# Softmax sums of a two-layer masked attention: summing layer 1's pair tiles by accumulating DMAs, layer 0's sums in place

## The chip, the cores and the metric

The kernel runs on one core of a Trainium2 chip. The metric is the device time of one execution in microseconds (us), the median of several runs. All tensors that matter here are float32.

## What is computed

Two attention layers on 16 graphs of 1024 nodes with 256 features. Each layer normalizes its input, applies ReLU, and adds a masked multi-head attention to it. Layer 0 has 4 heads of 64, layer 1 has 8 heads of 32 and biases.

```python
h = jnp.maximum(_layernorm(x), 0.0)
q, k, v = heads(h @ Wq), heads(h @ Wk), heads(h @ Wv)      # layer 1: + bq, bk, bv
scores = jnp.einsum('bhnd,bhmd->bhnm', q, k) / sqrt(D)
scores = jnp.where(adj > 0, scores, -inf)
w = jax.nn.softmax(scores, axis=-1)
x = x + concat(einsum('bhnm,bhmd->bhnd', w, v)) @ Wo + bo
```

## The kernel before

Scores are computed transposed: keys on the 128 partitions, 512 queries in the free dimension. A **step** is one tile `p` of 128 x 4 x 512 numbers: in layer 1 four heads against one block of 128 keys, in layer 0 two heads against two blocks. A **group** is the steps that share an output: 8 steps in layer 1, 4 in layer 0. There are two groups for each half of the queries, so a graph has 16 steps in layer 0 and 32 in layer 1, and the program has 768 in all. The list of steps goes through layer 0 of graph b+1 and then layer 1 of graph b, so that one graph's projections can be computed under the other's attention. In the text that follows, a is the first step of layer 0 of graph b+1 and c the first of layer 1 of graph b.

`Stream.run` writes the order of the work by hand, one loop turn i for each step:

- `scores(st)` on PE (TensorE): four matmuls into two PSUM pairs of a ring of three.
- `weigh` on PE, two steps later: four matmuls of `v` and `p` into `po`. In an even step that holds a large unit (`k`, `q`, `values`, `end_half`) it is put off to the odd step after it.
- `exponentials(st)`: for each half of the tile DVE (VectorE) applies the mask by a minimum (L388), and ACT (ScalarE) takes the exponential (L393). The tiles of odd steps have two buffers, those of even steps three.
- units that are due at this step: parts of the normalization of the next inputs (`stats`, `norm`, `add_bias`), the transposes (`turn`), the projections (`k`, `q`, `values`), the output projection (`end_half`, which fills `py`), and pieces of the mask (`load`, `flip`, `put`, `second`). `later(i, f)` gives a unit its step.

A softmax sum is taken by PE too: `count` multiplies a tile by a matrix of ones, so that the sum over the keys stands in all partitions of its head. To spend fewer matmuls, tiles are added first. In layer 1, `count_steps` lets POOL (GpSimd) add an odd step's tile to the even one before it (L502, 128 x 2048), and the sum is counted two steps later: four counts for a group. In layer 0, `add_tiles` adds a step's two halves into a tile `t` (DVE, for the first step POOL) and POOL adds the running sum (L418); the group is counted once.

When a group ends, `end_group` sets the steps of its end: `spread` (ACT copies the sum to `s`, SP sends it to DRAM as `sd` and back as `sn`, spread over the partitions), `invert` (DVE's reciprocal `vn`, and SP's DMAs that broadcast it as `inv`), `normalize` (POOL multiplies the output by it into `cat`) and `end_half` (PE). In layer 0 these are 2, 3, 5 and 7 steps after the group's last weigh, in layer 1 they are 2, 4, 7 and 9, and for a graph's last group 2, 3, 4 and 8. The program's last group has `hurry` set and a shorter end.

[...]

Of the kernel before, what the change touches and what calls it, by code (L numbers as in the profile page):

```python
# [18 lines left out]
P = 128  # L19
# [63 lines left out]
def fast_program(ctx, tc, a, w, loads, chk):  # L83
# [14 lines left out]
    small = ctx.enter_context(tc.tile_pool(name="small", bufs=4))  # L98
# [50 lines left out]
    class Inputs:  # L149
# [6 lines left out]
        def stats(self, half, tiles=range(4)):  # L156
# [10 lines left out]
            if 3 in tiles:  # L167
                ve = small.tile([P, 4], F32, tag="ve", name=f"ve_{n}")
                nc.gpsimd.tensor_scalar_add(ve, mv[:, :, 1], EPS)
                self.rstd[half] = small.tile([P, 4], F32, tag="rstd", name=f"rstd_{n}")  # L170
# [3 lines left out]
                self.shift[half] = small.tile([P, 4], F32, tag="shift", name=f"shift_{n}")  # L174
# [76 lines left out]
    class Group:  # L251


        def __init__(self, inp, mask, qh, g, half):
# [9 lines left out]
            self.hurry = False  # L264

# [113 lines left out]
    def exponentials(st, between):  # L379
# [4 lines left out]
        st.p = pp.tile([P, 4, 512], F32, tag=f"p{odd}", bufs=2 if odd else 3, name=f"p_{st.n}")  # L384
# [44 lines left out]
    class Stream:  # L429
# [19 lines left out]
        def run(self):  # L449
# [3 lines left out]
            for i in range(n + LEAD):  # L453
# [36 lines left out]
        def count_steps(self, i, st):  # L490


            gr = st.gr
            if st.j % 2 == 0 and not (gr.hurry and st.j == NT - 2):
                return
            if gr.hurry and st.j >= NT - 2:
                if st.last:
                    self.counted(i, gr)
                gr.count(st.p, False, st.last)
            else:  # L500
                one = self.steps[i - LEAD - 1].p
                nc.gpsimd.tensor_add(one, one, st.p)  # L502
                self.later(i + 2, gr.count, one, st.j == 1, st.last)
# [7 lines left out]
        def end_group(self, i, gr):  # L511
# [82 lines left out]
    for b in range(B):  # L594
# [4 lines left out]
        steps += layer_steps(inputs[1][b], masks[b])  # L599
    steps[-1].gr.hurry = True  # L600
# [23 lines left out]
    for b in range(B - 1):  # L624
        mine, a, c = inputs[1][b], first[b + 1], second[b]
        if b == 0:

            norms(mine, 0, a + 1, a + 2, a + 4, a + 5)
            half_inputs(mine, 0, a + 6, a + 8, a + 10, a + 12)
            norms(mine, 1, a + 9, a + 10, a + 12, a + 13)  # L630
            half_inputs(mine, 1, a + 15, c + 2, c + 6, c + 4)
        else:
            norms(mine, 0, a - 10, a - 9, a - 7, a - 6)
            half_inputs(mine, 0, a - 5, a + 2, a + 4, a + 6)
            norms(mine, 1, a - 8, a - 7, a - 5, a - 4)
            half_inputs(mine, 1, a - 3, a + 8, c + 6, c + 4)
        for kt in range(NT):
            later(a + 4 + kt, masks[b].second, kt)
        if b + 2 < B:
            other, mask = inputs[0][b + 2], masks[b + 2]  # L640
            later(a + 1, open_x, b + 2, 0)
            later(a + 10, open_x, b + 2, 1)
# [9 lines left out]
        else:  # L652
            last, e = inputs[1][b + 1], c + 32
            norms(last, 0, c + 1, c + 2, c + 4, c + 5)
            half_inputs(last, 0, c + 9, c + 12, c + 14, c + 16)
            norms(last, 1, c + 9, c + 10, c + 12, c + 13)
            half_inputs(last, 1, c + 17, c + 20, e + 6, e + 4)
            for kt in range(NT):
                later(c + 8 + 2 * kt, masks[b + 1].second, kt)
# [250 lines left out]
```

## Time and profile before

| | |
|---|---|
| median of 3 runs | 3377.5 us (3376.9 to 3377.79) |
| profiled execution, own time | 3380.06 us |
| its span, first to last instruction | 3378.3 us |
| granted TensorE clock | 0.998 |
| PE busy | 3339.0 us (99%) |
| DVE busy | 2501.1 us (74%) |
| POOL busy | 2447.1 us (72%) |
| ACT busy | 2182.5 us (65%) |
| DMA queues, share of 16 engines | SP's 12.6%, POOL's 6.3% |

A line of the groups reads: source line, engine, operation, output and inputs by the program's names, shapes and count, then busy time in us and the mean of one in ns, then the idle time of the engine just before, with what ended it. A line of a timeline reads: start and duration in us, engine, source line, operation, count, and in brackets the idle time before with what ended it. PEld are the weight loads, SPq is the DMA-issuing sequencer of SP. Each float32 matmul appears as two records.

### The profile page before, as it was taken

What the parts mean: (1) busy time and instruction counts of PE and PEld (TensorE: products, weight loads), DVE (VectorE), ACT (ScalarE), POOL (GpSimd) and SP (SyncE); (2) the same over time, 40 slices, a digit from 0 to 9 for tenths busy, and PEclk for the clock granted to TensorE, in tenths of its full rate; (3) what the DMA queues carried; (4) which work ended last, traced back from release to release, by engine and by line L of the source; (5) the groups of instructions that cost most, each with busy time, mean ns of one, the idle gap of its engine ahead of it and who ended that gap; (6) DMA issues with size and microseconds to landing.
All of it is one profiled execution on the core that took longest, in us unless ns stands there. A gap on an engine that the chain in (4) does not pass through costs nothing. (4 is left out here: it accounts for less than half of the span.)

```text
span 3378.3 us, 46298 instructions
## 1 busy us (share of the span) xinstructions
PE 3339.0 (99%) x18190; PEld 1298.6 (38%) x18190; DVE 2501.1 (74%) x2664; ACT 2182.5 (65%) x2402; POOL 2447.1 (72%) x1606
## 2 busy tenths in 40 slices
PE   8999999999999999999999999999999999999998
PEld 3443333333333333333334333333343333433432
DVE  4676767767677786777867778677786777777876
ACT  5567566675666756667566675666756667665665
POOL 5577778777677766877677686777867778676776
PEclk9999999999999999999999999999999999999999
DMA  6221111212112111121221212212121111210001
GB/s 131 48 42 36 48 39 36 51 36 47 36 36 51 42 42 36 39 48 42 45 39 36 48 39 48 39 39 45 39 47 37 48 39 36 51 38 18 14 17 31
DMA packets 250738, 141.77 MB, mean 42 GB/s; under 512 B 182416, under 2 KB 217488, under 8 KB 250512
## 3 DMA queue, kind: packets, MB, share of 16 engines
q1 hardware_dynamic: 232080, 105.18, 12.6%
q0 software_dynamic: 18432, 33.56, 6.3%
q8 instruction: 144, 2.36, 0.3%
q14 instruction: 82, 0.67, 0.1%
HBM read 120.33 MB, written 18.34 MB: 41 GB/s over the span
## 5 line engine op out<-in xcount | busy, mean ns | idle before, releaser
L393 ACT ACTIVATE p<-p 128x1024 f32<-128x1024 f32 x1536 | 1615.1, 1057 | 973.8 <-DVE p L388 931.7
L388 DVE SCALAR_TENSOR_TENSOR p<-mask,ps 128x1024 f32<-128x1024 fp8e4 x1536 | 1797.0, 1215 | 583.5 <-PE ps L372 553.8
L502 POOL TENSOR_TENSOR p<-p,p 128x2048 f32<-128x2048 f32 x255 | 1161.9, 4557 | 372.2 <-PE po L405 368.3
L372 PE MATMUL ps<-qT,kT 32*128 32x512 f32 (+1 forms) x6144 | 1145.6, 631 | 7.6 <-DVE p L388 4.9
L405 PE MATMUL po<-p,v 128*32 128x512 f32 (+1 forms) x6144 | 992.4, 601 | 0.4 <-ACT o L288 0.4
L418 POOL TENSOR_TENSOR t<-t,t 128x1024 f32<-128x1024 f32 x192 | 486.2, 2532 | 389.8 <-DVE t L416 341.6
L372 PEld LDWEIGHTS ps<-qT,kT 32*128 32x128 f32 (+1 forms) x6144 | 367.7, 184 | 675.7 <-issue 305.3
L405 PEld LDWEIGHTS po<-p,v 128*32 128x32 f32 (+1 forms) x6144 | 227.8, 118 | 689.4 <-issue 529.1
L416 DVE TENSOR_TENSOR t<-p 128x1024 f32<-128x1024 f32 x192 | 325.0, 1693 | 14.6 <-POOL t L418 14.4
L278 PE MATMUL pz<-p,ones 128*32 128x512 f32 x2056 | 267.8, 593 | 0.2 <-POOL p L502 0.2
L212 PE MATMUL pq<-hT,wk 128*128 128x512 f32 x512 | 240.7, 613 | 3.1 <-ACT hT L201 3.1
L353 PE MATMUL py<-wo,cat 128*128 128x256 f32 x1008 | 237.8, 387 | 4.7 <-POOL cat L324 2.8
L241 PE MATMUL pv<-wv,hT 128*128 128x256 f32 x1024 | 237.9, 385 | 0.1
L212 PE MATMUL pq<-hT,wq 128*128 128x512 f32 x512 | 236.6, 605 | 0.0
L241 PEld LDWEIGHTS pv<-wv,hT 128*128 128x128 f32 x1024 | 189.4, 190 | 71.7 <-issue 24.0
L353 PEld LDWEIGHTS py<-wo,cat 128*128 128x128 f32 x1008 | 185.4, 190 | 80.0 <-issue 33.4
L324 POOL TENSOR_TENSOR cat<-o,inv 128x512 f32<-128x512 f32 x127 | 164.5, 1296 | 10.3 <-DMA inv<-vd 9.3
L416 POOL TENSOR_TENSOR t<-p 128x1024 f32<-128x1024 f32 x64 | 165.0, 2578 | 2.8 <-ACT p L393 2.4
L358 DVE TENSOR_TENSOR x<-py,x 128x1024 f32<-128x1024 f32 x63 | 76.4, 1213 | 118.4 <-PE py L353 118.4
L190 POOL TENSOR_TENSOR x<-x,bo 128x1024 f32<-128x1024 f32 x64 | 152.6, 2385 | 1.5 <-DMA bo<-in_bo_dram 1.4
L212 PEld LDWEIGHTS pq<-hT,wk 128*128 128x128 f32 x512 | 93.5, 192 | 145.2 <-issue 120.1
L212 PEld LDWEIGHTS pq<-hT,wq 128*128 128x128 f32 x512 | 92.2, 189 | 139.8 <-issue 138.3
(51 smaller groups left out, 1635.4 us busy)
## 6 DMA issues: line engine op xcount, KB each, us to landing
adj<-in_adj_dram POOLq DMA_DIRECT2D x128, 256.0 KB, 3.6
x<-in_x_dram SPq DMA_DIRECT2D x32, 512.0 KB
inv<-vd SPq DMA_DIRECT2D x128, 128.0 KB
inv<-vd SPq DMA_DIRECT2D x252, 64.0 KB
out_dram<-x SPq DMA_DIRECT2D x31, 512.0 KB
adjT<-adj SPq DMA_TRANSPOSE x128
sd<-s SPq DMA_DIRECT2D x64, 4.0 KB
sn<-sd SPq DMA_DIRECT2D x64, 4.0 KB
```

The source lines that it names most:

```text
L212: nc.tensor.matmul(pq[:, m, :], wt[self.layer][:, c, ts(m, P)], self.hT[half][:, c, :], start=(c == 0), stop=(c == 1),)
L241: nc.tensor.matmul(pv[:, i, :], self.hT[half][:, c, ts(i, P)], w.v[self.layer][:, c, :], start=(c == 0), stop=(c == 1),)
L278: nc.tensor.matmul(self.s[r * self.D : (r + 1) * self.D, :], w.ones[:, : self.D], p[:, r, :], start=start, stop=stop,)
L324: nc.gpsimd.tensor_mul(self.half.cat[:, self.g, :], self.ob, self.inv)
L353: nc.tensor.matmul(py[:, i, :], self.half.cat[:, c, ts(i, P)], w.o[self.layer][:, c, :], start=(c == 0), stop=(c == 1),)
L372: nc.tensor.matmul(st.ps[i // 2][:, i % 2, :], gr.inp.kT[r * D : (r + 1) * D, gr.g, ts(kt, P)], gr.inp.qT[r * D : (r + 1) * D, gr.g, ts(gr ...
L388: nc.vector.scalar_tensor_tensor(out=half, in0=gr.mask.m[:, kt, ts(gr.qh, 512)].unsqueeze(1).to_broadcast([P, 2, 512]), scalar=BIG, in1=st ...
L393: nc.scalar.activation(half, half, AF.Exp, scale=gr.scale)
L405: nc.tensor.matmul(gr.o[r * D : (r + 1) * D, :], gr.inp.v[:, kt, h * D : (h + 1) * D], st.p[:, i, :], start=(kt == 0), stop=(kt == NT - 1),)
L416: engine.tensor_add(t, st.p[:, 0:2, :], st.p[:, 2:4, :])
L418: nc.gpsimd.tensor_add(t, t, gr.t)
L502: nc.gpsimd.tensor_add(one, one, st.p)
```

## The change

Layer 1: POOL adds each odd step's tile to the even one as before. Then every second pair sum is added to the one before it by a DMA that accumulates (issued on POOL), and the result is counted six steps after its last weigh: two counts for a group. `brief` is set for a graph's last group, and for both last groups of the program: there the first two pair sums are added and the others are counted singly. Tiles of even steps have five buffers now. The end of a layer 1 group that is not brief moves to 6, 7, 9 and 11 steps.

Layer 0: `add_tiles` takes two steps at once, at odd steps, and works in the tiles themselves; `t` is gone. The end of a group moves to 4, 5, 7 and 9.

Units of the normalizations and projections, and the mask's second pass, get other steps. Small tiles have two buffers, `rstd` and `shift` four.

```diff
-        st.p = pp.tile([P, 4, 512], F32, tag=f"p{odd}", bufs=2 if odd else 3, name=f"p_{st.n}")
+        st.p = pp.tile([P, 4, 512], F32, tag=f"p{odd}", bufs=2 if odd else 5, name=f"p_{st.n}")
...
-    def add_tiles(st):
-        gr = st.gr
-        t = work.tile([P, 2, 512], F32, tag="t", bufs=3, name=f"t_{st.n}")
-        engine = nc.vector if st.j else nc.gpsimd
-        engine.tensor_add(t, st.p[:, 0:2, :], st.p[:, 2:4, :])
-        if st.j:
-            nc.gpsimd.tensor_add(t, t, gr.t)
-        gr.t = t
+    def add_tiles(one, two):
+        a, b = one.p[:, 0:2, :], one.p[:, 2:4, :]
+        nc.vector.tensor_add(a, a, b)
+        engine = nc.vector if one.j else nc.gpsimd
+        engine.tensor_add(b, two.p[:, 0:2, :], two.p[:, 2:4, :])
+        nc.gpsimd.tensor_add(a, a, b)
+        if one.j:
+            nc.gpsimd.tensor_add(a, a, one.gr.t)
+        one.gr.t = a
...
-                one = steps[i - 1] if 1 <= i <= n else None
-                if one and one.gr.layer == 0:
-                    add_tiles(one)
+                if i % 2 and 3 <= i <= n and steps[i - 2].gr.layer == 0:
+                    add_tiles(steps[i - 3], steps[i - 2])
...
-            else:
+            elif j % 2:
                 one = self.steps[i - LEAD - 1].p
                 nc.gpsimd.tensor_add(one, one, st.p)
-                self.later(i + 2, gr.count, one, st.j == 1, st.last)
+                if gr.hurry:
+                    self.later(i + 2, gr.count, one, j == 1, False)
+                elif gr.brief and j > 4:
+                    self.later(i + 2, gr.count, one, j == 5, st.last)
+                elif j % 4 == 1:
+                    gr.pair = one
+                else:
+                    nc.gpsimd.dma_start(one, gr.pair, accum_op=ALU.add)
+                    self.later(i + 6, gr.count, one, not gr.brief and j == 3, st.last)
...
-                self.later(i + 2, gr.count_added)
-                at = 2, 3, 5, 7
+                self.later(i + 4, gr.count_added)
+                at = 4, 5, 7, 9
             else:
-                at = (2, 3, 4, 8) if gr.last else (2, 4, 7, 9)
+                at = (2, 3, 4, 9) if gr.brief else (6, 7, 9, 11)
...
         else:
-            norms(mine, 0, a - 10, a - 9, a - 7, a - 6)
-            half_inputs(mine, 0, a - 5, a + 2, a + 4, a + 6)
-            norms(mine, 1, a - 8, a - 7, a - 5, a - 4)
-            half_inputs(mine, 1, a - 3, a + 8, c + 6, c + 4)
-        for kt in range(NT):
-            later(a + 4 + kt, masks[b].second, kt)
+            norms(mine, 0, a - 15, a - 14, a - 12, a - 11)
+            half_inputs(mine, 0, a - 9, a + 2, a + 4, a + 6)
+            norms(mine, 1, a - 11, a - 10, a - 8, a - 7)
+            half_inputs(mine, 1, a - 5, a + 8, c, a + 12)
+
+        for i, kt in zip((2, 4, 8, 12, 16, 20, 24, 28), range(NT)):
+            later(c + i, masks[b + 1].second, kt)
...
-            norms(other, 0, a + 7, a + 8, a + 10, a + 11)
-            half_inputs(other, 0, a + 14, c + 10, c + 12, c + 14)
-            norms(other, 1, a + 15, c + 1, c + 3, c + 4)
-            half_inputs(other, 1, c + 15, c + 18, c + 20, c + 24)
+            if b == 0:
+                norms(other, 0, a + 8, a + 9, a + 10, a + 11)
+                half_inputs(other, 0, a + 13, c + 8, c + 10, c + 12)
+            else:
+                norms(other, 0, a + 11, a + 12, a + 13, a + 15)
+                half_inputs(other, 0, c + 1, c + 4, c + 8, c + 12)
+            norms(other, 1, c + 1, c + 2, c + 3, c + 5)
+            half_inputs(other, 1, c + (9 if b == 0 else 7), c + 16, c + 20, c + 24)
```

`norms(inp, half, ...)` gives the steps of its four pieces (statistics twice, normalization twice; the bias addition follows one step later), `half_inputs` those of `turn`, `k`, `q` and `values`. For graph 0 and for the last graphs the units move in the same way, to steps of their own.

More of the change, by code (lines that the diff above doesn't have):

```diff
@@ L97, in fast_program @@
     pp = ctx.enter_context(tc.tile_pool(name="pp", bufs=2))
-    small = ctx.enter_context(tc.tile_pool(name="small", bufs=4))
+    small = ctx.enter_context(tc.tile_pool(name="small", bufs=2))
     ps_s = ctx.enter_context(tc.tile_pool(name="ps_s", bufs=3, space=PSUM))
@@ L169, in stats @@
                 nc.gpsimd.tensor_scalar_add(ve, mv[:, :, 1], EPS)
-                self.rstd[half] = small.tile([P, 4], F32, tag="rstd", name=f"rstd_{n}")
+                self.rstd[half] = small.tile([P, 4], F32, tag="rstd", bufs=4, name=f"rstd_{n}")
                 nc.gpsimd.tensor_tensor(self.rstd[half], ve, w.mhalf, ALU.pow)
@@ L173, in stats @@
                 nc.gpsimd.tensor_scalar_mul(less, mv[:, :, 0], -1.0)
-                self.shift[half] = small.tile([P, 4], F32, tag="shift", name=f"shift_{n}")
+                self.shift[half] = small.tile([P, 4], F32, tag="shift", bufs=4, name=f"shift_{n}")
                 nc.gpsimd.tensor_mul(self.shift[half], less, self.rstd[half])
@@ L264, in __init__ @@
             self.hurry = False
+            self.brief = self.last
         def steps(self):
@@ L490, in count_steps @@
         def count_steps(self, i, st):
[L493 to L496, printed above, removed]
+            gr, j = st.gr, st.j
+            if gr.hurry and j >= NT - 2:
                 if st.last:
@@ L599, in fast_program @@
         steps += layer_steps(inputs[1][b], masks[b])
+    for st in steps[-2 * NT :]:
+        st.gr.brief = True
     steps[-1].gr.hurry = True
@@ L626, in fast_program @@
         if b == 0:
[L628 to L631, printed above, removed]
-        else:
-            norms(mine, 0, a - 10, a - 9, a - 7, a - 6)
-            half_inputs(mine, 0, a - 5, a + 2, a + 4, a + 6)
-            norms(mine, 1, a - 8, a - 7, a - 5, a - 4)
-            half_inputs(mine, 1, a - 3, a + 8, c + 6, c + 4)
-        for kt in range(NT):
-            later(a + 4 + kt, masks[b].second, kt)
+            norms(mine, 0, a + 3, a + 4, a + 6, a + 7)
+            half_inputs(mine, 0, a + 9, a + 10, a + 12, a + 14)
+            norms(mine, 1, a + 11, a + 12, a + 14, a + 15)
+            half_inputs(mine, 1, c + 1, c + 3, c + 6, c + 4)
+            for kt in range(NT):
+                later(a + 4 + kt, masks[b].second, kt)
+        else:
+            norms(mine, 0, a - 15, a - 14, a - 12, a - 11)
[4 more added lines that the diff above has]
+            later(c + i, masks[b + 1].second, kt)
         if b + 2 < B:
@@ L641, in fast_program @@
             later(a + 1, open_x, b + 2, 0)
[L642 to L646 removed]
+            later(a + 11, open_x, b + 2, 1)
+            if b == 0:
[6 more added lines that the diff above has]
+            half_inputs(other, 1, c + (9 if b == 0 else 7), c + 16, c + 20, c + 24)
             for t in range(NT):
@@ L653, in fast_program @@
             last, e = inputs[1][b + 1], c + 32
[L654 to L659, printed above, removed]
+            norms(last, 0, c + 3, c + 4, c + 6, c + 7)
+            half_inputs(last, 0, c + 9, c + 12, c + 16, c + 20)
+            norms(last, 1, c + 11, c + 12, c + 14, c + 15)
+            half_inputs(last, 1, c + 17, c + 24, e + 6, e + 4)
     stream.run()
```

## The prediction

> **What bounds the kernel now.** I read the page's busy shares first (PE 99%, DVE 74%, POOL 72%, ACT 65%; clock 0.998), then its groups:
>
> ```profile
> L388 DVE SCALAR_TENSOR_TENSOR p<-mask,ps 128x1024 f32<-128x1024 fp8e4 x1536 | 1797.0, 1215 | 583.5 <-PE ps L372 553.8
> L502 POOL TENSOR_TENSOR p<-p,p 128x2048 f32<-128x2048 f32 x255 | 1161.9, 4557 | 372.2 <-PE po L405 368.3
> L278 PE MATMUL pz<-p,ones 128*32 128x512 f32 x2056 | 267.8, 593 | 0.2 <-POOL p L502 0.2
> ```
>
> DVE and POOL wait for PE (553.8 and 368.3 us), PE for nobody. So an instruction taken from PE shortens the span as long as the other queues keep up. Do they? The timeline of a stretch without projections, PE:
>
> ```profile
> 3292.79 1.14 PE L372 MATMUL ps<-qT,kT 32*128 32x512 f32 x8
> 3293.86 1.07 PE L405 MATMUL po<-p,v 128*32 128x512 f32 x8
> 3294.85 1.57 PE L372 MATMUL ps<-qT,kT 32*128 32x512 f32 x8
> 3296.36 1.06 PE L405 MATMUL po<-p,v 128*32 128x512 f32 x8
> 3297.24 1.04 PE L278 MATMUL pz<-p,ones 128*32 128x512 f32 x8
> 3298.21 1.14 PE L372 MATMUL ps<-qT,kT 32*128 32x512 f32 x8
> ```
>
> An even and an odd step ("pair") take 5.4 us, of which the count is 0.97 (3297.24 to 3298.21). The second scores take 1.57, not 1.14: they wait for a PSUM pair. POOL's addition of such a pair takes 4.56, the DVE masks 4 x 1.15 = 4.6: three queues are within 0.8 us of each other there. With a projection (3.65 us, start to start) a pair takes 8.5.
>
> POOL, end of a batch:
>
> ```profile
> 1378.96 4.59 POOL L502 TENSOR_TENSOR p<-p,p 128x2048 f32<-128x2048 f32 x1
> 1383.48 2.42 POOL L190 TENSOR_TENSOR x<-x,bo 128x1024 f32<-128x1024 f32 x1
> 1385.99 0.29 POOL L318 TENSOR_SCALAR ok_is_ge<-sn 128x16 f32<-128x16 f32 x1
> ...
> 1387.37 4.55 POOL L502 TENSOR_TENSOR p<-p,p 128x2048 f32<-128x2048 f32 x1
> ```
>
> POOL runs without a gap there and is already late; bias addition (2.4) and tests (1.15) stand ahead of the next pair sum. DVE waits for that sum, because the odd steps' tiles have two buffers (the waits: "DVE p L388 <- POOL p L502", 27.6 us in 16 waits). Last, a softmax sum's way to the reciprocal (ACT, SP, DVE):
>
> ```profile
> 1278.66 0.56 ACT L296 COPY s<-pz 128x512 f32<-128x512 f32 x1
> ...
> 1279.25 0.49 SPq L298 DMA_DIRECT2D sd<-s  x1
> 1280.82 0.32 SPq L300 DMA_DIRECT2D sn<-sd  x1
> ...
> 1282.45 0.20 DVE L305 RECIPROCAL vn<-sn 128x8 f32<-128x8 f32 x1 [2.52 <-DMA sn<-sd]
> ```
>
> From the end of the copy to the reciprocal: 3.2 us, and DVE stood in front of it for 2.52.
>
> [...] L416 on DVE lasts 1.22 us alone and 2.27 beside POOL, 1.69 on average.
>
> **The change part by part.** A batch is 24 pairs: a to a+14 (layer 0), c to c+30 (layer 1). In a batch of the steady state (1 to 13; 208.4 us each by the starts of their scores):
>
> *Counts.* Three groups drop from 4 counts to 2, the fourth (brief) from 4 to 3: 7 x 0.97 = **6.8 us off PE**. In all 110 counts, 107 us. Most short pairs keep theirs and the projection pairs lose theirs (8.5 to 7.5).
>
> *Other steps for units and mask pieces.* PE's work is the same. Before, pair c lasted 11.05; in batch 14, where DVE isn't late, 9.38: 1.7 us that the new order removes, with about 0.4 at c+24. PE alone would then need 208.4 - 6.8 - 2.1 = 199.5.
>
> *Accumulating DMAs.* 110 issues on POOL behind the sum that they add to; the row of the adj loads says 0.62, [...] I take 0.75, bounds 0.6 to 2. Landing: the adj queue's 6.3% of 16 engines is 1.66 us per load of 512 KB read, 3.6 with the ends. Two sources of 1 MB are 4 x 1.66 + 1.9 = 8.5 us, bounds 6 to 15. The source's buffer is wanted again (five even tiles on) 11 us or more after the issue, the count comes later still: no wait at 8.5.
>
> *Layer 0 in place.* Same additions (DVE 192, POOL 256), now in clumps after odd steps; they wait for weigh, which PE has done by then. Between 0 and 1 us a batch through DVE contention; I take it inside c+2 below. SP issues as many DMAs as before, at other steps (0.3 to 1.3 us each, with gaps between them in its timeline); the small pools cost nothing, since rstd and shift keep four buffers.
>
> *What becomes late.* I followed the queues pair by pair. A mask of an odd step may start 3.5 us into a short pair, 5.9 into one with a projection; late by more than 0.5, it delays the next scores.
>
> - c+6: L0's sum is now copied at c+5 and inverted at c+6, in a short pair. Copy ends 2.5 into it (odd exponentials and hn are ahead on ACT), plus 3.2: reciprocal at 5.7, and the odd mask behind it on DVE at 5.9 instead of 3.7. A transpose (c+7) holds the third PSUM pair, so the next scores need both of its halves: 5.9 + 2.3 against 5.4: **2.8 us**. Same cause at a: 0.5.
> - c+18 to c+22: after the sum of c+17 POOL has 4.55 + 0.75 (DMA) + 1.15 (tests) + 1.95 (rstd) + 1.3 (cat) = 9.7 in a pair of 5.4: the next sum starts 4.3 late and holds the odd mask of c+21: 1.0. DVE's statistics (1.2 in each of four steps) fall into the two short pairs: 1.6 and 1.8. **4.4 us**.
> - c+28: the output projection waits for cat, behind 4.55 + 0.75 + 1.15 + 2.4 (bias) + 1.3 = 10.1 on POOL; PE is there after 6.9 + 1.07 = 8.0: **2.2 us**.
> - c+14, c+26, c+30: a short pair right after one without count: the sum ends 4.55 in, the mask could start at 3.5; 1.1 - 0.6: **0.5 each**.
> - c+2: mask piece, statistics, reciprocal and residual (0.8 + 1.2 + 0.2 + 1.2) between DVE's masks, which start 0.7 late after the additions: **1.2**.
>
> Sum 12.6. So a batch takes 199.5 + 12.6 = 212.1, **+3.7**, and 13 batches +48. The first and the last two (19 counts, 18 us) I take at 0: their short pairs without count are held by POOL (4.55 and its extras) near 5.4 as before. The profiled execution's own time is 3380.06; 3428. The median of the runs lies 2.6 below it: **3425**.
>
> **The rivals.**
>
> 1. *The queues keep up* (faster). The mechanism is the same slack at the odd mask: if waits come to less than 8.9 us a batch, the count pays. For it: before, the pairs c+22 and c+24 took both statistics and lost only 0.5, and POOL is idle 28% of the span. Against: the three POOL queues above are sums of measured rows. Half the waits: 205.8, 13 x -2.6 = -34: 3343; none at all: -134, 3243.
> 2. *The DMA lands late* (slower still). If the add costs as much as the reads, landing is some 15 us: the even masks and the counts wait 4 us or less behind seven DMAs a batch, about 6 us beyond the waits they hide: 13 x 5.7 = +74, 3500. For it: nothing before moves 1 MB[...].
> 3. *POOL pays 2 us an issue*: 7 x 1.25, a part of it in POOL's idle time: +2.5 a batch, 3458.
> 4. *No net effect*: waits of 8.9 +/- 0.5. A narrow case.
>
> **How the numbers follow.** Slower by my ledger, with the waits between 9.4 and 14: 0.60; DMA late or issue dear: 0.18; keeping up: 0.16; no effect: 0.06. A measurement of this kernel tells about 0.2% from no change. So faster 0.16, same 0.06, slower 0.78. Range 3345 to 3490: low at half the waits, high just short of a 15 us landing. The slower cases' own range is 3385 to 3490.
>
> **What would show it.** Right: L280 with some 1176 records of layer 1 in place of 2056; pairs with a projection and no count at 7.5; c+6 near 8.2 with DVE waiting for sn; py at c+28 waiting for cat; more of "DVE p <- POOL p"; PE's busy share below 99%. Wrong: PE still without waits (then near 3250), or the reciprocal ready before 4 us in c+6. DMA landings above 11 us, with even masks released by a DMA, would show rival 2; POOL's DMA row above 1 us rival 3.

## The result and the profile after

The changed kernel takes 3794.1 us (median of 4 runs, 3785.1 to 3817.8) where the kernel before takes 3377.5: a ratio of 1.124 (95% interval 1.120 to 1.129). The direction was forecast; of the 417 us only 48 were. The profiled execution took 3817.8 us, with a span of 3816.0.

From the page of the kernel after: busy shares, granted clock in slices of the span, three groups (the mask is L390 now, POOL's pair sum L503, the count L280), and the accumulating DMA with its median us from issue to landing:

```profile
PE 3505.1 (92%) x17310; PEld 1355.0 (36%) x17310; DVE 2498.3 (65%) x2664; ACT 2172.3 (57%) x2402; POOL 2508.3 (66%) x1716
...
PEclk9999989999999998999999999998999999999989
...
L390 DVE SCALAR_TENSOR_TENSOR p<-mask,ps 128x1024 f32<-128x1024 fp8e4 x1536 | 1799.7, 1214 | 997.2 <-PE ps L374 542.7
...
L503 POOL TENSOR_TENSOR p<-p,p 128x2048 f32<-128x2048 f32 x255 | 1169.9, 4607 | 401.7 <-PE po L407 332.4
...
L280 PE MATMUL pz<-p,ones 128*32 128x512 f32 (+1 forms) x1432 | 223.8, 615 | 2.2 <-POOL p L503 2.2
...
p<-p POOLq DMA_DIRECT2D x110, 1024.0 KB, 7.1
```

No engine has become the bound: every engine's share fell. PE's busy time nevertheless rose from 3339 to 3505 us, although 880 records of the count are gone. PE stands idle for 311 us (39 before), and some clock slices show 8. Before, all showed 9:

```profile
PEclk9999999999999999999999999999999999999999
```

The idle time before DVE's mask grew from 583.5 to 997.2 us, and PE's part of it did not grow (553.8 to 542.7). What else ends it, the view of waits says (engine, what it waited for, us, times, longest):

```profile
DVE p L390 <- PE ps L374: 542.7, 326, 5.0
...
DVE p L390 <- DMA p<-p: 427.1, 92, 7.2
...
PE ps L374 <- DVE p L390: 156.5, 72, 6.1
```

A new row of 427 us: the mask of an even step waits for an accumulating DMA, six times in a batch (c+12, c+16, c+20, c+24, c+28 and the next a), 4.6 us each. PE waits for the mask in turn; before, that row of the groups had 4.9 us:

```profile
L372 PE MATMUL ps<-qT,kT 32*128 32x512 f32 (+1 forms) x6144 | 1145.6, 631 | 7.6 <-DVE p L388 4.9
```

One of these waits in the timeline of the kernel after, at c+16 (start, duration):

```profile
1474.42 0.90 POOL L511 DMA_DIRECT2D p<-p  x1 [0.30 <-POOL p L503]
...
1475.55 1.14 PE L374 MATMUL ps<-qT,kT 32*128 32x512 f32 x8
...
1481.91 2.35 DVE L390 SCALAR_TENSOR_TENSOR p<-mask,ps 128x1024 f32<-128x1024 fp8e4 x2 [5.41 <-DMA p<-p]
...
1483.19 3.21 PE L374 MATMUL ps<-qT,kT 32*128 32x512 f32 x8 [2.87 <-DVE p L390]
...
1486.33 3.53 PE L407 MATMUL po<-p,v 128*32 128x512 f32 x16
```

DVE is free from 1476.5 and the scores are there at 1476.7; the buffer for the masked tile is free when the DMA lands, 7.5 us after its issue. PE waits 2.87 us. And then its work itself is slow: scores of 3.21 us where 1.14 is usual (a part of it waits for the mask's second half), two weighs of 3.53 us where 1.92 is usual. The busy time by stretches of two microseconds (sum, PE's busy time and records, granted clock, DMA share, GB/s) shows why:

```profile
1478.00:1480.00 2.00, 2.00 (x6) 1.00 0.96 197
1480.00:1482.00 2.00, 0.32 (x1) 1.00 0.79 120
1482.00:1484.00 2.00, 0.81 (x2) 0.70 0.52 93
1484.00:1486.00 2.00, 2.00 (x8) 0.50 0.03 3
1486.00:1488.00 2.00, 2.00 (x10) 0.50 0.11 36
1488.00:1490.00 2.00, 2.00 (x16) 0.60 0.52 145
1490.00:1492.00 2.00, 2.00 (x18) 1.00 0.58 91
```

Around this wait TensorE's clock record stands at 0.50 for 6.8 us (1482.78 to 1489.61). Over the span it has 394 us at half clock (15 before). PE was at work in 359 of them. If work at half clock takes twice its time, some 180 us of them are lost (an estimate, half of the 359; 3.5 before); the two weighs above took 3.53 us for 1.92.

In a batch of the steady state (1 to 13) PE's record splits the loss as follows: 27.6 us more are 17.0 of idle time, 11.3 of work slowed by half clock (half of PE's busy time at half clock) and 5.3 of longer records of scores at full clock, which the prediction's view of the second scores (1.57 us for 1.14) lets one read as waits for a PSUM pair; the missing counts take 6.0 off. Outside these batches the changed kernel loses another 79 of the 438 us between the two profiled executions. This is bookkeeping from the records: how much of the slow clock would come back as time is another question (e8).

Where it is lost, in mean us from the start of an even step's scores to those of the next even step, over batches 1 to 13 (kernels of the experiments beside it):

| pair | before | after | e1 | e4 | e9 | e18 |
|---|---|---|---|---|---|---|
| a | 6.68 | 12.03 | 6.68 | 6.68 | 6.96 | 6.98 |
| a+2 to a+14 | 75.18 | 77.59 | 79.05 | 79.04 | 76.03 | 76.03 |
| c | 11.03 | 11.32 | 11.31 | 11.32 | 9.66 | 9.67 |
| c+2 | 5.51 | 13.97 | 13.86 | 8.89 | 7.53 | 7.40 |
| c+4, c+6 | 16.99 | 15.91 | 15.86 | 15.61 | 19.19 | 15.48 |
| c+8 | 8.50 | 10.85 | 10.66 | 11.66 | 8.86 | 8.51 |
| c+10 to c+14 | 26.50 | 22.73 | 21.51 | 21.52 | 24.79 | 24.78 |
| c+16 | 5.36 | 13.56 | 7.63 | 7.63 | 5.37 | 5.37 |
| c+18 | 8.49 | 5.49 | 10.36 | 10.19 | 7.63 | 7.63 |
| c+20, c+22 | 13.84 | 19.05 | 15.71 | 17.03 | 12.98 | 12.99 |
| c+24 | 8.99 | 10.75 | 9.87 | 9.56 | 15.32 | 9.84 |
| c+26 to c+30 | 21.29 | 22.78 | 21.74 | 21.75 | 20.62 | 23.01 |
| batch | 208.38 | 236.01 | 224.23 | 220.87 | 214.95 | 207.69 |

### The profile page after: what moved, and what is told of

Its sections match the earlier page's. It is cut to its first block, busy times and chain, and to the rows that moved or that the text cites. A ratio compares the mean times of both kernels' runs of the same rounds, so it can differ in the third digit from the quotient of the medians.

```text
span 3816.0 us, 44831 instructions
## 1 busy us (share of the span) xinstructions
PE 3505.1 (92%) x17310; PEld 1355.0 (36%) x17310; DVE 2498.3 (65%) x2664; ACT 2172.3 (57%) x2402; POOL 2508.3 (66%) x1716
## 3 DMA queue, kind: packets, MB, share of 16 engines
q1 hardware_dynamic: 232080, 105.18, 11.3%
## 5 line engine op out<-in xcount | busy, mean ns | idle before, releaser
L390 DVE SCALAR_TENSOR_TENSOR p<-mask,ps 128x1024 f32<-128x1024 fp8e4 x1536 | 1799.7, 1214 | 997.2 <-PE ps L374 542.7
L503 POOL TENSOR_TENSOR p<-p,p 128x2048 f32<-128x2048 f32 x255 | 1169.9, 4607 | 401.7 <-PE po L407 332.4
L374 PE MATMUL ps<-qT,kT 32*128 32x512 f32 (+1 forms) x6144 | 1277.6, 651 | 158.1 <-DVE p L390 156.5
L407 PE MATMUL po<-p,v 128*32 128x512 f32 (+1 forms) x6144 | 1044.2, 639 | 6.2 <-ACT o L290 6.1
L374 PEld LDWEIGHTS ps<-qT,kT 32*128 32x128 f32 (+1 forms) x6144 | 406.5, 189 | 915.3 <-DVE p L390 405.2
L420 POOL TENSOR_TENSOR p<-p 128x1024 f32<-128x1024 f32 x128 | 303.1, 2368 | 310.2 <-DVE p L419 305.1
L355 PE MATMUL py<-wo,cat 128*128 128x256 f32 x1008 | 274.6, 430 | 85.2 <-ACT hT L201 75.8
L419 POOL TENSOR_TENSOR p<-p 128x1024 f32<-128x1024 f32 x64 | 151.1, 2361 | 302.4 <-DVE p L416 293.7
L355 PEld LDWEIGHTS py<-wo,cat 128*128 128x128 f32 x1008 | 211.1, 216 | 173.3 <-ACT hT L201 69.4
L280 PE MATMUL pz<-p,ones 128*32 128x512 f32 (+1 forms) x1432 | 223.8, 615 | 2.2 <-POOL p L503 2.2
L416 DVE TENSOR_TENSOR p<-p 128x1024 f32<-128x1024 f32 x128 | 185.9, 1452 | 0.0
L290 ACT COPY o<-po 128x512 f32<-128x512 f32 x128 | 74.3, 580 | 188.5 <-PE po L407 119.0
L422 POOL TENSOR_TENSOR p<-p,p 128x1024 f32<-128x1024 f32 x64 | 151.4, 2366 | 5.0
```

Source lines behind the costliest of these rows:

```text
L280: nc.tensor.matmul(self.s[r * self.D : (r + 1) * self.D, :], w.ones[:, : self.D], p[:, r, :], start=start, stop=stop,)
L355: nc.tensor.matmul(py[:, i, :], self.half.cat[:, c, ts(i, P)], w.o[self.layer][:, c, :], start=(c == 0), stop=(c == 1),)
L374: nc.tensor.matmul(st.ps[i // 2][:, i % 2, :], gr.inp.kT[r * D : (r + 1) * D, gr.g, ts(kt, P)], gr.inp.qT[r * D : (r + 1) * D, gr.g, ts(gr ...
L390: nc.vector.scalar_tensor_tensor(out=half, in0=gr.mask.m[:, kt, ts(gr.qh, 512)].unsqueeze(1).to_broadcast([P, 2, 512]), scalar=BIG, in1=st ...
L407: nc.tensor.matmul(gr.o[r * D : (r + 1) * D, :], gr.inp.v[:, kt, h * D : (h + 1) * D], st.p[:, i, :], start=(kt == 0), stop=(kt == NT - 1),)
L416: nc.vector.tensor_add(a, a, b)
```

## The experiments

All times are medians. The kernel before, run on the same chip as each set, had medians of 3376.9 to 3377.9 us. In the experiments the source lines after the mask's tile stand 7 lower where the buffers are taken in turn (mask L397, pair sum L510, accumulating DMA L518).

### What the waits for the DMA cost (e1, e2, e3)

**e1_rotate**, the five buffers strictly in turn:

```diff
+    evens = [0]
...
-        st.p = pp.tile([P, 4, 512], F32, tag=f"p{odd}", bufs=2 if odd else 5, name=f"p_{st.n}")
+        if odd:
+            tag = "p1"
+        else:
+            tag = f"p0{evens[0] % 5}"
+            evens[0] += 1
+        st.p = pp.tile([P, 4, 512], F32, tag=tag, bufs=2 if odd else 1, name=f"p_{st.n}")
```

> The changed kernel with one edit: the five buffers of the even steps' tiles are taken strictly in turn, so the source of an accumulating DMA is overwritten five even tiles later and not four. Theory 1 (the loss is DVE's wait for the DMA that still reads the buffer it is about to fill, 427 us in 92 waits, and what follows from it): these waits all but vanish (under 30 us), the pairs c+12, c+16, c+20, c+24, c+28 and a get shorter by some 22 us a batch together, time 3440 to 3540. Theory 2 (the moved units and the late sums are the loss; the DMA wait only takes the place of a wait that would be there anyway): the waits turn up as waits for PE, POOL or sn, time above 3700.

Measured: 3630.0 us, 164 less than the changed kernel. The view of DVE's waits in e1 has no row for the DMA any more; of the kernel's masks and reciprocals it says

```profile
DVE p L397 <- PE ps L374: 533.9, 385, 5.0
DVE vn L307 <- DMA sn<-sd: 192.0, 88, 6.7
...
DVE p L397 <- POOL p L510: 28.7, 59, 2.4
```

The granted clock rises from 0.948 to 0.966. So the order of the buffers is shown to cost 164 us, and theory 2, in which the waits would come back elsewhere, falls for that part. The forecast of 3440 to 3540 is missed: c+18, which had been short while DVE was late before it, is 10.36 us long now, and c+2 is as before.

Why the order mattered: the tiles' addresses in the program show that the pool gives out the buffer that was released first. A DMA's source is released by the DMA itself, five steps after its tile was begun, its destination by the count, nine steps after; the next source is released before the last destination. So in layer 1 a source's buffer comes back after four even tiles (c+4, c+12, c+20 and c+28 have one, c+8, c+16 and c+24 another), a destination's after six (c+2 and c+14). After four even tiles it is wanted 2.0 to 4.8 us after the DMA's issue (means by pair, c+12 to the next a); in e1, after five, 11.0 us or more, when the DMA has landed.

**e2_single**, no accumulating DMA:

```diff
...
-                elif j % 4 == 1:
-                    gr.pair = one
-                else:
-                    nc.gpsimd.dma_start(one, gr.pair, accum_op=ALU.add)
-                    self.later(i + 6, gr.count, one, not gr.brief and j == 3, st.last)
+                at = 4 if not gr.brief or (j == 1 and not gr.hurry) else 2
+                self.later(i + at, gr.count, one, j == 1, st.last)
...
-                at = (2, 3, 4, 9) if gr.brief else (6, 7, 9, 11)
+                at = (2, 3, 4, 9) if gr.brief else (4, 7, 9, 11)
```

> The changed kernel without accumulating DMAs: each pair sum is counted by itself, four steps after its addition (two in the last groups), and the group's sum copied four steps after its last tile; five buffers, moved units and layer 0 in place stay. Theory 1: no DVE wait for a DMA; the cost of the moves stays (c+2 and c+8 long) and 7 counts of 0.97 us a batch come back, so 3500 to 3600. Theory 2: over 3650. If only the DMAs cost anything at all: at or below the kernel before, 3377.

Measured: 3562.3 us. As theory 1 has it: with no DMA at all and all counts back, the rest of the change keeps the kernel 185 us above the one before (c+2 at 13.5 us, c+8 at 11.4). That rest is the moved units, the moved ends and layer 0 in place; the last alone costs 28 us (e10).

**e3_no_dma** leaves out `dma_start`, and with it nearly half of layer 1's tiles in the sums (110 of 256 pairs); 1.0 is added to the sums as they are copied:

```diff
-            nc.scalar.copy(s, self.s)
+            nc.scalar.activation(s, self.s, AF.Identity, bias=w.ones[:, 0:1])
...
-                    nc.gpsimd.dma_start(one, gr.pair, accum_op=ALU.add)
```

> The changed kernel with the accumulating DMA left out and nothing in its place: half of layer 1's tiles are missing from the softmax sums there (1.0 is added to the sums in their copy so that their reciprocals stay finite). Counts, their steps and the order of buffers are those of the changed kernel. Theory 1 (only the wait for the buffer costs): within 1% of the kernel with buffers in turn. Theory 3 (issue on POOL, 21% of the DMA engines and SBUF traffic cost as well): lower than that one by 2% or more.

Measured: 3575.5 us, 1.5% below e1, between the two forecasts. So beside the wait for the buffer the DMAs cost about 55 us, their 100 us of issuing on POOL (110 x 0.91) included. The pairs that differ most are c+18 (7.70 for 10.36) and a+2 (12.92 for 14.45), and DVE's waits for `sn` are 155 us for 192: at a+2 DVE stands 3.9 us in front of the reciprocal in e1, at a+1 2.1 in e3. The sums' own way through DRAM is slower beside the accumulating DMAs; e9 below shows the extreme.

### The moved units (e4, e6) and the reciprocals (e5, e7, e12)

At c+2 PE waits 4 us, and its clock stands at 0.50 from 1414.52 to 1421.34 us. The timeline of the kernel after, POOL, ACT and PE:

```profile
1407.59 2.38 POOL L190 TENSOR_TENSOR x<-x,bo 128x1024 f32<-128x1024 f32 x1
1409.92 2.25 POOL L326 TENSOR_TENSOR cat<-o,inv 128x512 f32<-128x512 f32 x1
...
1412.21 0.58 ACT L290 COPY o<-po 128x512 f32<-128x512 f32 x1 [3.85 <-POOL cat L326]
...
1415.15 1.02 ACT L201 COPY hT<-ph 128x1024 f32<-128x1024 f32 x1
...
1416.22 6.02 PE L355 MATMUL py<-wo,cat 128*128 128x256 f32 x15 [3.92 <-ACT hT L201]
```

`o` has two buffers: ACT's copy of a group's result waits for `cat` of two groups before. `cat` used to run three steps ahead of that copy, with layer 0's late sums it runs one step ahead, and stands behind the bias addition on POOL. The copy waits 3.85 us, and what stands behind it on ACT starts after it, among it the copy of the transpose (at 1415.15), which gives back the PSUM pair that `py` needs.

**e4_rotate_cat**, on e1:

```diff
-                at = 4, 5, 7, 9
+                at = 4, 5, 6, 9
```

> Buffers in turn, and besides the normalization of layer 0's groups one step earlier (6 steps after the last weighing in place of 7). Theory: pair c+2 (14.0 us against 5.5 before) is long because ACT's copy of a group's result waits for the cat of two groups before, which now runs one step ahead of it in place of three. Then c+2 gets shorter by 3 to 6 us, and the time is 40 to 80 us below that with buffers in turn alone. If the cause is another (the statistics, the mask piece or the additions on DVE): within 15 us of it.

Measured: 3580.2 us, 50 less than e1, as the theory had it; c+2 goes from 13.86 to 8.89. The chain is shown.

**e6_turn_earlier**, on e4 (shown for one of the three):

```diff
-            half_inputs(mine, 0, a - 9, a + 2, a + 4, a + 6)
+            half_inputs(mine, 0, a - 7, a + 2, a + 4, a + 6)
```

> Buffers in turn and earlier normalization of layer 0, and besides the three transposes in c+7, c+23 and c+27 moved to c+13, c+25 and c+29, so that no step with a projection follows them. Theory: PE's 0.8 us at c+8, 1.35 at c+24 and 1.9 at c+28 are waits for the copy of the transpose, which holds the third PSUM pair; they go, with the slow clock behind them: 3 to 5 us a batch, 3510 to 3545. Rival: c+28 waits for cat on POOL and keeps its 1.9: 3550 to 3570.

Measured: 3523.7 us, 57 less than e4, inside the forecast. PE's idle time falls from 1.25 to 0.3 us at c+24 and from 1.9 to 0.3 at c+28. A transpose in an odd step takes the third PSUM pair into the next step; a projection there finds none. But the sum came out right in part by luck: c+8 didn't get shorter (11.66 and 11.69 us), c+26 got 0.9 longer, and 3.3 of the 4.9 us a batch came at c+18 and a+2, which the forecast didn't name.

**e5_recip_later**, on e4, and **e7_both**, the two together:

```diff
-                at = 4, 5, 6, 9
+                at = (4, 6, 8, 9) if gr.last else (4, 5, 6, 9) if gr.g else (4, 6, 7, 9)
             else:
-                at = (2, 3, 4, 9) if gr.brief else (6, 7, 9, 11)
+                at = (2, 4, 5, 9) if gr.brief else (6, 8, 9, 11) if gr.g else (6, 8, 10, 11)
```

> Buffers in turn and earlier normalization of layer 0, and besides every reciprocal two steps after its sum's copy, not one, wherever a later step is open (layer 0's second group of the first half keeps one). Theory: the waits at a+2 (1.2 us), c+8 (1.4) and c+18 (1.6) stand behind a reciprocal on DVE that waits for sn, and TensorE's clock is halved for 3 to 7 us after those at c+8 and c+18, another 6 us a batch. So 8 to 10 us a batch less: 3450 to 3490. Rival: DVE's masks are late there from the statistics and mask pieces; then under 2 us a batch, 3555 to 3580.

> Both edits of the last two together: reciprocals later and transposes moved. If the two are independent, their gains add: 3390 to 3445. If PE is then never idle long enough for its clock to be halved, a batch comes near PE's own work of 201 us and the kernel beats the one before: under 3370.

Measured: 3579.0 and 3595.4 us; the gains that were forecast didn't come. The first lies in the range of its rival, but not for the rival's reason. Where the reciprocal was in front of the mask, the theory held: c+18 fell from 10.19 to 6.05, c+8 from 11.66 to 9.96. But c+10 rose from 8.51 to 15.68: `cat` of layer 0's last group now stood in c+9 behind a pair sum and a DMA on POOL, and `py` of c+10 waited 4.0 us for it. What was won in several pairs was lost in one.

**e12_recip_where**, on e6, the later reciprocal only where `cat` isn't pushed behind a pair sum:

```diff
-                at = 4, 5, 6, 9
+                at = (4, 6, 7, 9) if gr.last else (4, 5, 6, 9)
...
-                at = (2, 3, 4, 9) if gr.brief else (6, 7, 9, 11)
+                at = (2, 4, 5, 9) if gr.brief else (6, 7, 9, 11) if gr.g else (6, 8, 10, 11)
```

> The kernel with buffers in turn, earlier normalization and transposes moved, with the reciprocal a step later only in the groups where it stood in front of masks and cat still runs before a pair sum on POOL: layer 0's last group (normalized 7 steps after its last weighing), layer 1's first group of each half, and the brief groups. Theory: c+18 loses 2 us, c+8 1, a+2 0.2, and c+10 stays at 8.7: some 3 us a batch under the kernel with transposes moved (3524), 3475 to 3500. If c+10 gets long again, cat waits for inv on POOL: above 3524.

Measured: 3511.4 us, 12 less than e6, short of the forecast: c+18 lost 2.3 us and c+8 1.4, and c+10 took 2.7 back: 1.43 us of it (13 times) its scores wait, not for `cat` this time, but for the PSUM pair that DVE's copy of `qT` still holds. A steady batch gained nothing (215.94 and 215.85 us); the 12 us come from batch 0, which takes 229.5 us for 241.6.

### The clock (e8)

**e8_fill_pe**, useless matmuls where PE waits, on e4:

```diff
+        if b:
+            fills[c + 8] = steps[c].gr
+            halves[c + 18] = steps[c + 8].gr
+            later(c + 24, steps[c + 16].gr.fill)
```

> Buffers in turn and earlier normalization of layer 0, and besides useless work for PE where it waits: four matmuls of 0.97 us together, into the idle softmax-sum bank, ahead of the scores of c+8, between the two halves of c+18's, and ahead of the projection in c+24; nothing else moves. Clock theory (the cost of a wait is in good part the halved clock after it): the slow matmuls of c+8 and c+18 (3 us each) mostly go, the time falls by 2 to 5 us a batch, 3515 to 3555, though PE has 2.9 us a batch more to do. If only the waits themselves cost time: the same or up to 1 us a batch more, 3575 to 3600.

Measured: 3580.1 us, as e4. By the time the second theory is right, and the forecast gain was not there. In a steady batch of the two profiled executions the filler put in 3.0 us of work; PE's idle time fell by 2.75 us, the work slowed by half clock by 2.6 (granted clock 0.985 for 0.973), and the scores' waits inside their records grew by 1.1. So nearly all of the filler lay in time that was idle anyway, and of the slow clock that it took away little came back as time: 1.1 us a batch in these two executions, nothing in the medians. That work is slow at half clock, the records show (two weighs of 3.53 us for 1.92 above); that every microsecond of it lengthens the kernel, no experiment here shows.

### The accumulating DMA at the old steps (e9, e10, e11)

**e9_old_steps**: units, mask pieces and layer 0's ends as in the kernel before, but for two transposes that come two steps later; buffers in turn; and

```diff
-                    self.later(i + 6, gr.count, one, not gr.brief and j == 3, st.last)
+                    self.later(i + (6 if gr.brief else 4), gr.count, one, not gr.brief and j == 3, st.last)
...
-                at = (2, 3, 4, 9) if gr.brief else (6, 7, 9, 11)
+                at = (2, 3, 4, 8) if gr.brief else (4, 6, 9, 11)
```

> Accumulating DMAs in the schedule of the kernel before: units, mask pieces and layer 0's end at the old steps, buffers in turn, layer 0 in place. A pair-of-pairs sum is counted four steps after its last tile was weighed, the group's sum copied then and inverted two steps later, the output projection of the first half in c+28 and the two transposes before it two steps later. Theory (the DMAs' idea pays; what cost the time were the buffer order, the moved units and the halved clock after their waits): PE's own work is 201 us a batch, with 2 to 6 us of waits 203 to 207 against 208.4 before: 3310 to 3365. Rival (POOL cannot carry issue and sums in short pairs, DVE and clock follow, whatever the steps): above 3400.

**e10_in_place**: the same without DMAs, with transposes, counts and ends as before, so that only layer 0's additions (and the buffers) differ from the kernel before.

> The kernel before with layer 0's sums in place and five buffers in turn, nothing else: no accumulating DMA, all units, counts and ends at the old steps. Theory (in-place sums cost 0 to 1 us a batch): 3370 to 3395. Rival (additions in clumps after odd steps delay DVE's masks): above 3400.

**e11_old_steps_pool**: e9 with the tile line of the changed kernel.

> As the kernel with DMAs in the old steps, but the five buffers given out by the pool as in the changed kernel (the first released is the first taken). Theory (buffer order alone is worth what it was worth in the changed kernel, 164 us): 130 to 190 us above its twin with buffers in turn, with a DVE wait for DMA p<-p of some 400 us. Rival (only the changed schedule made the wait expensive): within 60 us of its twin.

Measured: 3480.7, 3405.8 and 3482.7 us: e9 and e10 in the ranges of their rivals. The moves of units and of the ends, done for the new sums, cost more than they gave: with the old steps the DMA version is 313 us faster than the changed kernel, and 149 faster than e1, which has the same order of buffers. In-place sums alone cost 28 us (ratio 1.0082, 1.0065 to 1.0099): c+2 takes 7.41 us for 5.51 and c+4 9.90 for 8.50, while c is 1.4 shorter. At c+3 and c+5 the counts wait for POOL's sums (0.57 and 1.12 us). The forecast for e11 failed in a useful way: the pool's order costs nothing there, and no mask waits for a DMA. Counted two steps earlier, a destination is released in time, and the tiles' addresses show the five buffers strictly in turn in layer 1. The program of the changed kernel with this one step alone moved (`i + 6` to `i + 4`) gives the same addresses in layer 1; no run timed it. So the bad order came from the count's step, not from the pool as such.

e9's worst pair is c+24 (15.3 us). Its timeline, POOL, SP, DVE and PE:

```profile
2021.81 0.90 POOL L518 DMA_DIRECT2D p<-p  x1 [0.30 <-POOL p L510]
...
2022.57 0.35 SPq L302 DMA_DIRECT2D sn<-sd  x1
...
2030.23 0.25 DVE L307 RECIPROCAL vn<-sn 128x16 f32<-128x16 f32 x1 [3.88 <-DMA sn<-sd]
...
2031.61 2.25 PE L374 MATMUL ps<-qT,kT 32*128 32x512 f32 x8 [2.57 <-DVE p L397]
```

The read of `sn`, 8 KB, is issued 0.8 us after the accumulating DMA and takes 7.6 us, where the list of DMAs of the kernel after has 1.6 as the median. The packet record shows that it runs among the DMA's packets of 8 KB (2023.3 to 2029.5): its 128 packets of 64 bytes come in eight groups some 0.6 us apart, and a packet of 8 KB takes 0.65 us. The adj load issued between the two isn't the cause, its packets begin at 2029.0. DVE stands 3.88 us in front of the read, and PE 2.57 behind DVE. The next two weighs (2033.80) take 1.92 us: in this batch no half clock follows the wait.

### Taking the rest away (e13 to e18)

**e14_recip_dma**, on e9:

```diff
-                at = (2, 3, 4, 8) if gr.brief else (4, 6, 9, 11)
+                at = (2, 3, 4, 8) if gr.brief else (4, 8, 9, 11)
```

> As the kernel with DMAs at the old steps, with one edit: layer 1's reciprocals eight steps after the last weighing instead of six. Theory: c+24 loses 6 to 7.5 us a batch, but cat now waits on POOL for the later inv, so that up to 2 of it come back: 3390 to 3430. Rival: c+24 keeps more than 12 us: above 3450.

**e13_best**, on e9:

```diff
-                at = 2, 3, 5, 7
+                at = (2, 4, 5, 7) if gr.last else (2, 3, 5, 7)
...
-                at = (2, 3, 4, 8) if gr.brief else (4, 6, 9, 11)
+                at = (2, 4, 5, 8) if gr.brief else (4, 8, 10, 13)
...
-            half_inputs(mine, 0, a - 3, a + 2, a + 4, a + 6)
+            half_inputs(mine, 0, a - 5, a + 2, a + 4, a + 6)
```

> Accumulating DMAs at the old steps, buffers in turn, and every reciprocal placed so that DVE doesn't stand behind a read that an accumulating DMA holds up: layer 1 eight steps after the last weighing (four after the copy), layer 0's last group and the brief groups one step later than before, the first half's output projection in c+30. Theory: c+24 falls from 15.3 to about 8 us, c+6 from 11.5 to about 8, c+28 by 1 to 2: 201 to 204 us a batch, 3295 to 3345, faster than the kernel before. Rival (POOL's queue, or the statistics on DVE between short pairs, hold c+20 to c+30): 3400 to 3470.

Measured: 3452.7 and 3426.3 us. In both c+24 fell (to 9.7 and 9.8 us), which settles the delayed read; both times missed their forecasts and lie in the ranges of their rivals, since c+28 grew by 2.6 in e14 (`cat` later) and c+6 stayed at 11.7 in e13. There, in e13's timeline, it isn't the reciprocal that holds DVE, but POOL:

```profile
1925.02 9.01 POOL L510 TENSOR_TENSOR p<-p,p 128x2048 f32<-128x2048 f32 x2
...
1929.58 2.35 DVE L397 SCALAR_TENSOR_TENSOR p<-mask,ps 128x1024 f32<-128x1024 fp8e4 x2 [5.34 <-POOL p L510]
...
1930.85 1.13 PE L374 MATMUL ps<-qT,kT 32*128 32x512 f32 x4 [1.37 <-DVE p L397]
```

Ahead of the pair sum at 1925.02 stand layer 0's in-place sums, `rstd`, an adj load, tests and `cat`.

**e15_pool_order**, on e13, and **e16_stats_early**, on e15:

```diff
-                at = (2, 4, 5, 7) if gr.last else (2, 3, 5, 7)
+                at = (2, 4, 5, 7) if gr.last else (2, 3, 5, 7) if gr.g or not gr.qh else (2, 3, 6, 7)
...
-            self.later(i + at[1] + 1, gr.test)
+            self.later(i + at[1] + (1 if gr.layer or gr.g or not gr.qh else 3), gr.test)
...
-            half_inputs(mine, 0, a - 5, a + 2, a + 4, a + 6)
+            half_inputs(mine, 0, a - 4, a + 2, a + 4, a + 6)
# e16 besides:
-            norms(mine, 0, a - 10, a - 9, a - 7, a - 6)
+            norms(mine, 0, a - 12, a - 11, a - 9, a - 8)
```

> As the last kernel (DMAs at the old steps, reciprocals later), with POOL's small work at the border of the layers moved behind the first pair sum of layer 1: the third layer-0 group is tested and normalized in c+3, not c+1 and c+2, and the transpose of c+27 is in c+28. Theory (POOL's queue holds the mask at c+6): c+6 falls from 11.7 to about 8 us, c+26 by 1, 3355 to 3385, no slower than the kernel before. Rival (in-place additions on DVE, late counts): c+6 above 10.5, 3410 to 3430.

> The same, with the statistics of layer 1's first half in c+20 and c+21, not c+22 and c+23. Theory (DVE's statistics in the short pair hold the second mask and so the scores): c+22 and c+24 together lose 1 to 2 us of 14.3, 15 to 25 us below its twin. Rival: they only move the wait to c+20: within 8 us of its twin.

Measured: 3409.0 and 3429.3 us; the first lies above its forecast, the second 20 us above its twin, outside both of its ranges. In e15 c+6 fell to 7.82 as expected, and the next wait appeared two steps on: `py` at c+8 (9.5 to 11.3 us) for a `cat` behind the bias addition on POOL. In e16 c+24 lost 1.1 us and c+30 took 2.4: the statistics only moved the wait, to another pair.

**e17_border** and **e18_last**, on e15, share the first line:

```diff
-        later(at[3] + 1, inp.add_bias, half)
+        later(at[3] + (5 if half and not inp.layer and inp.b > 1 else 1), inp.add_bias, half)
# e17 besides:
-                at = (2, 4, 5, 8) if gr.brief else (4, 8, 10, 13)
+                at = (2, 4, 5, 8) if gr.brief else (6 if gr.qh and not gr.g else 4, 8, 9 if gr.g else 10, 13)
# and the third group's count at i + 6; e18 instead:
-            self.later(i + at[1] + (1 if gr.layer or gr.g or not gr.qh else 3), gr.test)
+            self.later(i + at[1] + (3 if (gr.layer and gr.g and not gr.qh) or (not gr.layer and gr.qh and not gr.g) else 1), gr.test)
```

> As the kernel with POOL's small work moved, with the bias addition of layer 0's second half four steps later, the count and sum of the third layer-1 group six steps after its last weighing, and cat of the second group one step earlier. Theory (order of POOL's queue): c+8 falls from 11.3 to about 9, c+28 and c+30 together by 2 to 3: 3345 to 3375, the first version under the kernel before. Rival (POOL's load itself is the bound there): the waits move to other pairs, 3395 to 3415.

> As the kernel with POOL's small work moved (3409 us), with only the bias addition of layer 0's second half four steps later and the tests of layer 1's second group two steps later. Theory (order of POOL's queue): c+8 falls from 11.3 to 8.5 as it did, c+30 from 10.3 to about 9, 3 to 4 us a batch less: 3357 to 3372, just under the kernel before. Rival (POOL's load): c+30 or c+28 gets longer again, 3380 to 3400.

Measured: 3455.5 us, above both ranges of e17, and 3359.9, inside e18's forecast. The later bias took c+8 to 8.5 in both. In e17 `cat` in c+26 went ahead of a pair sum, that sum came late, and c+30 took 15.6 us; in one batch `py` takes 5.66 us there, where 3.72 is usual. e18 is the first version that beats both kernels, the one before by half a percent: ratio 0.9946 (0.9932 to 0.9959). From its page:

```profile
PE 3276.2 (97%) x17310; PEld 1274.5 (38%) x17310; DVE 2430.2 (72%) x2664; ACT 2177.1 (65%) x2402; POOL 2538.0 (76%) x1716
...
L397 DVE SCALAR_TENSOR_TENSOR p<-mask,ps 128x1024 f32<-128x1024 fp8e4 x1536 | 1795.1, 1214 | 650.4 <-PE ps L374 516.9
L402 ACT ACTIVATE p<-p 128x1024 f32<-128x1024 f32 x1536 | 1612.7, 1056 | 937.6 <-DVE p L397 895.3
L510 POOL TENSOR_TENSOR p<-p,p 128x2048 f32<-128x2048 f32 x255 | 1170.0, 4610 | 159.1 <-PE po L414 69.9
...
L280 PE MATMUL pz<-p,ones 128*32 128x512 f32 (+1 forms) x1432 | 218.7, 599 | 30.6 <-DMA p<-p 17.0
```

PE is at 97%, its busy time 63 us below before, and the granted clock is 0.995. A steady batch is 0.7 us shorter (207.69 against 208.38): the counts take 5.6 us less, but 3.2 go to PE's waits, 1.0 to half clock and 0.7 to longer scores. The last line shows what is still open: in 18 places a count itself waits for the accumulating DMA, 17.0 us in all, most of them at c+29.

## Why the prediction was wrong

The sign was right, and so were the prices of the new operation; the size was wrong by a step about buffers and by missing terms. The first alone doesn't explain the miss: with it set right, e1 at 3630 us still lies 205 above the forecast and outside its range.

- **"The source's buffer is wanted again (five even tiles on) 11 us or more after the issue: no wait at 8.5."** This is the step that failed. The landing was 7.1 us (8.5 taken), the issue 0.91 us on POOL (0.75 taken), both within their bounds. The 11 us were right too: in e1, where the buffer does come back after five even tiles, it is wanted 11.0 us or later. But in the changed kernel it comes back after four, and at c+16 it was wanted 2 us after the issue. That made 92 waits of 4.6 us and 164 us of the time (e1). The prediction took "five buffers" for "five tiles on" and never asked which buffer the pool gives out. Its 8.5 us were an estimate from the adj load's 1.66 us; that the reading of two tiles sets the time, and not the adding, was the author's assumption, and no run here tells the two apart.
- **The price of a wait.** The ledger charged a wait at its length. In e1, where the DMA's waits are gone, PE is idle for 12.8 us in a batch, and the ledger's waits summed to 12.6, though at partly other pairs, so that the agreement is luck. The batch took 224.2 and not 212.1. Of the other 12, by PE's record, 6.5 are work slowed by half clock, 2.9 are waits inside the scores' records, and 2.5 are work that the ledger had taken off too freely (units and counts, below). The clock record shows 0.50 in stretches of 3.41 and 6.83 us; how long PE stood idle before them is in the last section. The kernel before hardly showed this: three stretches, none in a steady batch. This term is a reading of the records; e8 did not turn it into time.
- **Other steps for units: 2.1 us a batch less.** They cost instead. The same DMAs with the same order of buffers at the old steps are 149 us faster (e9 against e1), and two single corrections to the moved steps were worth 50 and 57 us (e4, e6). Of the 1.7 us at c, 1.4 come without any move of units, with layer 0 in place and the five buffers (e10, 9.61 for 11.03).
- **c+2: 1.2.** The pair was 8.5 us longer than before. It was mis-sized by a wait that wasn't looked for: ACT's copy of `o` behind `cat` (e4). With that taken away PE waits 1.17 us there and the pair takes 8.89; the prediction's 7.5 and 1.2 make 8.7.
- **c+6: 2.8.** The mechanism was right (the reciprocal one step after the copy holds the mask); PE waits 2.1 us at c+6 and c+8 together, and the half clock behind costs 1.7 more at c+8. The way of the sum was taken at 3.2 us; beside an accumulating DMA it is longer (7.6 us for one read in e9).
- **c+18 to c+22: 4.4, from POOL's backlog and the statistics.** In e1 these three pairs take 26.1 us; the prediction's short pairs of 5.4, one pair of 8.5 and the 4.4 make 23.7. The cause was another: with the reciprocal a step later c+18 falls from 10.2 to 6.05 (e5). POOL's backlog was real, but showed at the border of the layers (e13, e15). The sign that the prediction named for it, more of "DVE p <- POOL p", wasn't there in the changed kernel: 20.8 us for 27.6.
- **c+28: 2.2.** The size was right (1.85 us of idle) by luck: most of it was a transpose's PSUM pair (e6), and `py` waited 0.26 us for `cat`.
- **Layer 0 in place, 0 to 1 us a batch, "they wait for weigh, which PE has done by then".** Alone it costs 2.2 us a batch (e10, 210.55 against 208.38): the additions end a step later, and at the border of the layers the counts wait for POOL.
- **a, c+14, c+26, c+30: 0.5 each.** No such waits: in e1 PE has none at a, c+14 and c+30 and 0.1 at c+26.
- **The 6.8 us of counts.** The records are gone as forecast (L280 1432, of which 1176 of layer 1). But a count was priced at 0.97 us from start to start; a pair without its count is 0.86 shorter (e9: c+22 4.50 for 5.36, c+18 7.63 for 8.49), which makes 6.0 us a batch.
- **The first and the last two batches: 0.** Batch 0 takes 251.3 us for 219.3, batch 14 233.4 for 202.6, and what follows 143.9 for 122.2; with the beginning, 6 us shorter, this is 79 us. In e1 it is still 45. The cause stays open.
- **The rivals.** Rival 2 named the sign that was seen, "even masks released by a DMA", and gave the wrong reason: the DMA isn't late, the buffer is early. Its 3500 is also well below 3794. Rival 3, 2 us an issue, is refuted by the measured 0.91. The end of rival 1, 3243 with no wait, is far from what the repairs reached (3360).

## What to carry to other kernels

Before a transfer is given a buffer, follow the buffer: with a pool that hands out what was released first, a tile that is released early (a DMA's source) comes back earlier than the number of buffers suggests (here after four tiles with five buffers), and moving the release of its neighbour by two steps can put that right. When PE is the bound, give slow clock a line of its own in the sum of waits: in e1 12.8 us of waits a batch went with 6.5 us of slowed work. And before units are moved, write down for each engine's queue what then stands ahead of the instruction that PE waits for next.

## What the runs showed of the hardware

- TensorE's clock: the changed kernel's record has 78 stretches at 0.50 of the clock, 394 us in all, most of them 3.41 or 6.83 us long. All 78 begin on one grid of 3.413 us, to within 3 ns over the whole span. Of the grid's windows at full clock in batches 1 to 13, 34 had 2.0 us or more without a matmul in PE's record, and half clock followed each; of 79 with 0.65 to 2.0 us it followed 30, and it followed none of the 692 with less. A wait can fall into one window or be split over two: single waits of 2.5 us had no half clock after them.
- The changed kernel's five executions lie in the order of their clock, from 3785.1 us at 0.960 to 3817.8 at 0.948; all executions of the kernel before lie between 3376.3 and 3380.6, at 0.997 to 0.999. Which of the two, time or clock, drives the other isn't shown.
- The accumulating DMA of two 1 MB tiles lands 7.1 us after its issue (6.9 to 9.2), 7.1 to 8.0 in the experiments' medians (a single one took 14 us in e1, one 22 in e4), and costs POOL 0.87 to 0.96 us.
- A read of 8 KB on SP's queue that was issued 0.8 us behind it took 7.6 us (e9). Seven reads of 4 KB in the changed kernel that were issued 0.3 to 0.6 us behind one took only 1.6 to 1.8: the first of their packets began ahead of the first 8 KB packet (259.78 against 259.86 us in one), and all 128 within 0.5 us.
